# Router ranks from one subtraction, sums that are shared, and a new order for a Mamba and mixture-of-experts layer

## The chip, the cores and the metric

The kernel runs on one core of a Trainium2 chip, as one program of some 14,000 instructions. The core has five engines that run side by side, each with its own queue of instructions in a fixed order: TensorE (PE in the profile, with its weight loads as PEld), VectorE (DVE), ScalarE (ACT), GpSimd (POOL) and SyncE (SP), which here only starts transfers. An engine takes its queue in order, so an instruction that waits holds everything behind it on that engine. TensorE writes its results into PSUM, the small accumulator memory; everything else lies in SBUF, the working memory of 128 partitions, or in device memory. The metric is the device time of one execution in microseconds (us).

## The reference

The layer takes x of 4 sequences x 1024 tokens x 128 features in float32. It has two halves, each followed by a residual sum and a layer normalization.

```python
# first half: a selective state-space mixer (Mamba), per sequence
xr, z = split(x @ W_in.T)                       # 256 channels each
xs    = silu(causal_conv4(xr) + conv_b)
dt_r, b, c = split(xs @ W_x.T)                  # 64, 16, 16
dt    = softplus(dt_r @ W_dt.T + b_dt)
h_t   = exp(dt_t * a) * h_{t-1} + (dt_t * x_t) * b_t   # 16 states for each channel
y_t   = sum_s(h_t * c_t) + D * x_t
x     = layernorm(x + (y * silu(z)) @ W_out.T)
# second half: 8 experts, the best 2 for each token
scores = x @ Wr + br
weights = softmax over the two largest scores   # the lower index wins a tie
out    = sum_e weights[e] * (gelu(x @ W1[e] + b1[e]) @ W2[e] + b2[e])
x      = layernorm(x + out)
```

## The kernel before

**Units and rounds.** The tokens are cut into ten units (`UNITS`, line 42): pieces of one sequence of 512 tokens, at the start two of 256, at the end one of 384 and one of 128. A unit is handled as chunks of 128 tokens, n of them (4, 3, 2 or 1). The first nine units make eight sparse rounds for the experts (`ROUNDS`; round 0 has the two units of 256, each other round one unit, so rounds 1 to 6 have 512 tokens and round 7 has 384); the last unit of 128 tokens is dense: it goes through all eight experts.

**The mixer.** For each unit `project`, `select` and `softplus` make the inputs of the scan. Then `step` (line 802) runs 16 times, once for each state: TensorE spreads b over the partitions (line 824), VectorE multiplies it with dt*x (line 861), ScalarE makes the decay a (line 847), VectorE runs the recurrence with one scan for each half of the channels (line 880), POOL multiplies the result h with c (line 895, tile hc) and TensorE adds it up in y (line 905). h has 2 buffers and hc has 3, so a scan can wait for POOL's product of an earlier step. `finish_mixer` (line 949) gates y, projects it, normalizes it into the tile acc, has SP copy acc into a second tile, twin (line 1017), and computes the router scores.

**Router.** Still in `finish_mixer`, and all on VectorE: `score` (line 1056) adds the bias and takes the largest score of each token. `ranks` (line 1067) compares all 8 x 8 pairs of scores of a token: greater, or equal with the other's index lower (the constant triangle `before`). Four operations make a 0 or 1 for each pair, a sum over the 8 others gives each expert's rank, and ranks 0 and 1 give the mask. `weigh` (line 1096) takes the exponentials (ScalarE, line 1093) times the mask, sums them, takes the reciprocal, and multiplies. `most` and `first_only` belong to the way the bias b1 is folded into W1: row 0 of the transposed tokens is replaced by ones.

**Dispatch.** `dispatch` (line 1128) works on a round. TensorE counts tokens for each expert; `blocks` (line 1172, VectorE) turns the counts into blocks of 128 slots, with running sums over the 8 experts made from a product with the triangle `upto` and a sum, and finds which expert owns each block; `places` (line 1201) finds the slots of each token's best and second expert, with a product and a sum for each; `weights` (line 1230) does the same for the two router weights and writes them as a 129th column of acc (best) and twin (second). Then POOL scatters each chunk twice, acc by the best slot and twin by the second, into a slot table in device memory (line 1262, two scatters for a chunk, eight for a round of 512 tokens). The slot tables are set to zero once near the start, by four transfers from SP (`clear`, line 506).

**Experts.** `experts` (line 1322) loads four blocks of 128 slots at a time (xb), transposes them on TensorE, copies them to SBUF as xq, multiplies with W1 (line 1290), applies gelu on ScalarE (line 1303), multiplies with W2 (line 1314), scales with the weight column into yb and stores them. A round of 512 tokens has 15 blocks, round 7 has 13. For rounds below `LATE` the copy xq (line 1350) and the scaling yb (line 1426) run on ScalarE, for the others on VectorE (lines 1359 and 1428). `combine` gathers the two results of each token with an indirect DMA of POOL that adds into acc (line 1495), `store` normalizes and writes. `dense` does the last unit.

**What sets the order.** Every piece of work is put into a `Plan` (line 77) with an engine, an estimated cost, what it reads and writes, a place (in units of one step of 512 tokens) and an urgency. `order` (line 147) simulates the engines with these costs and sorts all pieces into one list; the queues follow this list. The constants in lines 22 to 49 are places, urgencies and switches of this planner: `B_AT` to `BC_URG` place the step's parts, `PREP` to `SSTEP` and `PREP_OF` the preparation of a unit, `D_AT` and `D_OF` the dispatch, `X_AT` and `X_OF` the experts, `C_AT` and `C_OF` the combining, `Z_AT` the clearing of the slot tables, `W1_AT` and `W2_AT` the fetch of the expert weights. Work marked `port=True` on VectorE and POOL is planned one at a time; for work marked `beside` (POOL's scatters and gathers) `BESIDE` and `PATIENCE` (lines 27 and 28, read in lines 185 to 189) say when it may be started:

```python
if op["beside"] and needy:
    if port[0] == "DVE" and max(t, port[1]) <= port[2] - BESIDE:
        t = max(t, port[1])
    else:
        t = max(t, known + PATIENCE)
```

## Time and profile before

| | |
|---|---|
| median of 16 runs | 796.25 us (794.18 to 798.0) |
| the profiled execution: its own time / its span | 798.54 us / 796.8 us |
| TensorE busy | 658.7 us (83%), 4594 matmuls |
| VectorE busy | 657.5 us (83%), 1036 instructions |
| ScalarE busy | 558.0 us (70%), 843 instructions |
| GpSimd busy | 532.6 us (67%), 637 instructions |
| TensorE clock granted, mean | 0.912 of full |
| last scan ends | at 733.9 us of the span |

The profile gives busy times by engine and by groups of instructions (line of the kernel, engine, operation, output<-input, shape, count, busy us, mean ns of one), tables of busy time by stretch of the span, who waited for whom, a timeline of each engine, and the chain of work that ended last, followed back from the end. A busy share is a mean over stages with different limits; a wait counts only on the engine that sets the end of its stage. A busy TensorE in these records is not one at its peak, since its matmuls are pipelined.

### The profile page before, as it was taken

The numbers are of one execution on the slowest core, as the hardware profiler recorded it, in microseconds if no ns is written. First come the engines' busy times: TensorE is split into PE (matmuls) and PEld (weight loads), VectorE is DVE, ScalarE is ACT, GpSimd is POOL, SyncE is SP. The second block draws the span as 40 slices with busy tenths as digits, with TensorE's granted clock in tenths as the row PEclk, the third lists the DMA queues.
The fourth block names the chain that finished last, engine by engine and source line by source line (L and its number), as shares of the span: only waits on it lengthen the run. The fifth ranks groups of instructions, "written<-read, shape, count | busy, mean of one in ns | idle before, by whom it ended". The sixth has DMA issues, their size and how long they took to land. (4 is left out here: it accounts for less than half of the span.)

```text
span 796.8 us, 14284 instructions
## 1 busy us (share of the span) xinstructions
PE 658.7 (83%) x4594; PEld 563.0 (71%) x4594; DVE 657.5 (83%) x1036; ACT 558.0 (70%) x843; POOL 532.6 (67%) x637
## 2 busy tenths in 40 slices
PE   5557838669997999799987996999789988888885
PEld 4446526358875987598766874988588977777784
DVE  2698998999989998999989989998979997984322
ACT  2853865827867886778777888787867867675553
POOL 4356545576656897479938795769686886975604
PEclk9765967859997999889998998899999999999998
DMA  6952313347424664266524633555355555566652
GB/s 190 232 144 56 104 46 102 106 126 230 142 60 127 191 175 118 67 172 183 140 66 128 203 75 116 155 179 161 81 155 175 140 148 177 144 144 178 149 160 36
DMA packets 106120, 109.20 MB, mean 137 GB/s; under 512 B 9640, under 2 KB 72152, under 8 KB 106048
## 3 DMA queue, kind: packets, MB, share of 16 engines
q1 hardware_dynamic: 94384, 99.44, 43.4%
q0 software_dynamic: 11248, 8.33, 5.9%
q8 instruction: 38, 0.62, 0.3%
q10 hardware_dynamic: 416, 0.53, 0.2%
q14 instruction: 34, 0.28, 0.1%
HBM read 87.96 MB, written 18.27 MB: 133 GB/s over the span
## 5 line engine op out<-in xcount | busy, mean ns | idle before, releaser
L895 POOL TENSOR_TENSOR hc<-h,cc 128x512 f32<-128x512 f32 (+3 forms) x320 | 358.1, 1219 | 158.7 <-DVE h L880 34.0
L905 PE MATMUL y<-ident,hc 128*128 128x128 f32 x1024 | 172.7, 293 | 49.7 <-POOL hc L895 47.5
L880 DVE TENSOR_TENSOR_SCAN h<-a,state,u 128x512 f32<-128x512 f32 (+3 forms) x192 | 185.4, 1000 | 20.4 <-POOL hc L895 7.3
L847 ACT ACTIVATE a<-dt,nega 128x1024 f32<-128x1024 f32 (+3 forms) x160 | 152.9, 974 | 66.2 <-DVE h L880 60.2
L861 DVE TENSOR_TENSOR u<-dtx,u 128x1024 f32<-128x1024 f32 (+3 forms) x160 | 162.2, 1014 | 22.9 <-PE u L824 10.7
L905 PEld LDWEIGHTS y<-ident,hc 128*128 128x128 f32 x1024 | 124.8, 149 | 78.1 <-POOL hc L895 72.2
L1314 PE MATMUL ph<-w_sb,ht 128*128 x944 | 131.5, 292 | 24.3 <-ACT ht L1303 24.2
L1314 PEld LDWEIGHTS ph<-w_sb,ht 128*128 128x128 f32 x944 | 121.7, 206 | 28.7 <-ACT ht L1303 28.3
L880 DVE TENSOR_TENSOR_SCAN h<-a,u 128x512 f32<-128x512 f32 (+1 forms) x128 | 132.9, 1074 | 10.1 <-POOL hc L895 3.6
L1290 PE MATMUL ph<-xq,w 128*128 128x128 f32 x944 | 125.8, 283 | 15.4 <-DVE pick L1233 3.2
L243 ACT ACT_TABLE_LOAD x105 | 134.7, 1283 | 3.6 <-PEq L1657 1.8
L1290 PEld LDWEIGHTS ph<-xq,w 128*128 128x128 f32 x944 | 116.2, 197 | 21.3 <-issue 6.4
L1495 POOL DMA_INDIRECT acc<-ys_slots,slot_i x62 | 97.9, 1579 | 41.8 <-DVE acc L1555 24.5
L824 PE MATMUL u<-ident,bt 128*128 128x128 f32 x512 | 89.4, 290 | 10.6 <-DVE h L880 10.6
L1303 ACT ACTIVATE ht<-ph 128x512 f32<-128x512 f32 x118 | 66.0, 597 | 23.6 <-PE ph L1290 22.7
L824 PEld LDWEIGHTS u<-ident,bt 128*128 128x128 f32 x512 | 65.2, 148 | 20.7 <-DVE h L880 13.3
L1426 ACT ACTIVATE yb<-ph,xb 128x128 f32<-128x128 f32 x105 | 37.2, 363 | 46.9 <-PE ph L1314 42.4
L1262 POOL DMA_INDIRECT xs_slots<-acc,slot_i x31 | 33.8, 1090 | 46.9 <-DVE twin L1241 13.2
L613 PE MATMUL pxc<-xt,taps 128*128 128x512 f32 (+3 forms) x160 | 61.2, 531 | 3.2 <-ACT xt L603 2.6
L613 PEld LDWEIGHTS pxc<-xt,taps 128*128 128x128 f32 x160 | 30.1, 203 | 24.8 <-issue 17.5
L745 ACT ACTIVATE sq<-ex,shift 128x1024 f32<-128x1024 f32 (+3 forms) x40 | 38.0, 973 | 7.2 <-DVE q L753 6.5
L1262 POOL DMA_INDIRECT xs_slots<-twin,slot_i x31 | 35.6, 1149 | 6.8 <-issue 5.7
(140 smaller groups left out, 709.7 us busy)
## 6 DMA issues: line engine op xcount, KB each, us to landing
w<-w_dram SPq DMA_DIRECT2D x118, 256.0 KB, 3.1
cc<-cd SPq DMA_DIRECT2D x96, 256.0 KB, 3.5
xb<-xs_slots SPq DMA_DIRECT2D x24, 258.0 KB, 3.8
ys_slots<-yb SPq DMA_DIRECT2D x24, 256.0 KB, 2.4
cc<-cd SPq DMA_DIRECT2D x32, 128.0 KB, 2.9
cc<-cd SPq DMA_DIRECT2D x16, 192.0 KB, 3.1
w_sb<-in_w_dram SPq DMA_DIRECT2D x8, 256.0 KB, 4.8
w_own<-in_w_dram SPq DMA_DIRECT2D x8, 256.0 KB, 4.9
```

Source lines behind the costliest of these rows:

```text
L243: load(table)
L613: nc.tensor.matmul(pp()[:, :t_n], taps[:, k, c * P : (c + 1) * P], xt()[:, k : k + t_n], start=(k == 0), stop=(k == KC - 1),)
L824: nc.tensor.transpose(u_sb[:, bank, k * P : (k + 1) * P], bt()[:, k, s : s + 1].to_broadcast([P, P]), ident,)
L847: lambda: nc.scalar.activation(a()[:, :, :t_n], dt()[:, :, :t_n], AF.Exp, scale=nega[:, s : s + 1]),
L861: nc.vector.tensor_tensor((u_sb[:, 1:3, :t_n] if bank else u_sb[:, 1::-1, :t_n]), dtx()[:, :, :t_n], u_sb[:, bank : bank + 1, :t_n].to_bro ...
L880: nc.vector.tensor_tensor_scan(h()[:, c, :t_n], a()[:, c, :t_n], u_sb[:, (1, bank)[c], :t_n], 0.0 if first == 0 else carry()[:, s, c : c + 1],
L895: nc.gpsimd.tensor_tensor(hc()[:, c, :t_n], h()[:, c, :t_n], cc()[:, :t_n], ALU.mult)
L905: nc.tensor.matmul(y()[:, k, c * P : (c + 1) * P], hc()[:, c, k * P : (k + 1) * P], ident, is_transpose=True, start=False, stop=(s == NS - 1),
L1262: ins = nc.gpsimd.indirect_dma_start(out=rd["xs"]()[:, :], out_offset=bass.IndirectOffsetOnAxis(ap=slot_i()[:, k, st["chunk"] + c : st["ch ...
L1290: nc.tensor.matmul(ph()[:, k * P : (k + 1) * P], w()[:, k * P : (k + 1) * P], xt()[:, width], start=True, stop=True, skip_group_check=True,)
L1314: nc.tensor.matmul(py, ht[:, k, :], w2_sb[:, bass.ds(e, 1), k * DM : (k + 1) * DM].rearrange("p o d -> p (o d)"), start=(k == 0), stop=(k ...
L1495: nc.gpsimd.indirect_dma_start(out=acc()[:, c, :DM], out_offset=None, in_=ys()[:, :], in_offset=bass.IndirectOffsetOnAxis(ap=slot_i()[:, k ...
```

## The change

- `ranks`: the difference other - own is taken once and compared with a constant `least`, which is 0 where the other's index is lower and the smallest normal number elsewhere. That replaces greater, equal, product and sum: two operations for four. The tile eq goes.
- `weigh`: compares the rank itself with 2 instead of reading the mask, and puts the reciprocal of the sum straight into the weight column of acc: the best expert's exponential is exp(0) = 1, so its weight is the reciprocal. It now writes a part of acc.
- `blocks`: the running sums over 8 experts come from one scan (times one, plus the count) instead of a product with `upto` and a sum. `upto` goes, a tile of ones comes.
- `places`: the two products go into one tile, and one sum covers both slots.
- `weights`: only the second weight is left, one product and one sum for each unit.
- `LATE` goes from 7 to 6: round 6 too has its xq copies and its output scaling on VectorE.
- The planned costs of these pieces and most constants of the planner are other numbers: a new order of all queues.

```diff
@@ -23,21 +23,21 @@
 GATHER, SCATTER = 1.85, 1.35
 N_B = 2
 SCAN_ORDER = 1, 0
-B_AT, B_URG = 3.6, 29.9
-BESIDE = -6.2
-PATIENCE = 0.2
+B_AT, B_URG = 4.3, 38.4
+BESIDE = -3.0
+PATIENCE = -3.9
 N_RUSH = 0
-X_AT, X_STEP, X_URG, C_AT, C_URG, D_AT = 1.9, 2.66, 6.2, 4.0, -1.0, -1.9
-A_AT, A_URG, BC_AT, BC_URG = -0.8, -2.3, 4.2, 15.8
-PREP, SEL, SOFT, SSTEP = 25.4, 5.3, -0.1, 2.7
-L_URG = -1.0
-URG, URG2, URG3, URG4 = 52.0, 191.1, 18.3, 0.8
-Z_AT, W2_AT, W1_AT, W1_STEP = 11.2, 0.0, 6.8, 3.5
-
-PREP_OF = (-6.7, -1.0, -10.0, 9.5, 1.2, 0.0, -3.0, 5.6, -5.2, 6.9, -3.9, 3.0)
-D_OF = (7.9, -3.5, -6.5, 3.3, 6.5, 4.7, -8.1, 5.3, 4.5, 1.7)
-X_OF = (-1.9, -7.6, 2.1, 1.3, 0.5, 0.4, 0.8, -16.1, 6.0, -2.5)
-C_OF = (-0.2, 5.0, -3.5, -1.3, 8.3, 3.3, 21.1, -2.6, 2.7, 9.1)
+X_AT, X_STEP, X_URG, C_AT, C_URG, D_AT = 2.0, 2.67, 6.2, 2.3, -0.7, -5.0
+A_AT, A_URG, BC_AT, BC_URG = -3.9, -0.9, 2.6, 13.8
+PREP, SEL, SOFT, SSTEP = 25.4, 8.6, -1.6, 7.4
+L_URG = 0.2
+URG, URG2, URG3, URG4 = 61.4, 108.8, 18.4, 1.7
+Z_AT, W2_AT, W1_AT, W1_STEP = 25.9, 0.4, 6.8, 3.1
+
+PREP_OF = (-10.5, 3.7, -10.0, 9.5, 2.6, 0.1, -1.2, 5.6, -5.2, 6.9, 2.2, 1.3)
+D_OF = (7.9, -1.6, -6.5, -9.3, 2.6, 3.6, -8.5, 5.0, 5.0, 1.7)
+X_OF = (-0.7, -10.0, 2.1, 1.3, 0.5, 0.4, 2.3, -10.7, 4.2, -7.3)
+C_OF = (4.2, 6.7, -4.4, -7.9, 5.2, 3.4, 22.2, -1.9, 1.2, 9.4)
 
 UNITS = [
     (0, 0, 256), (0, 256, 256), (0, 512, 512), (1, 0, 512), (1, 512, 512), (2, 0, 512), (2, 512, 512), (3, 0, 512), (3, 512, 384), (3, 896, 128),
@@ -46,8 +46,10 @@
 
 DENSE = [(9,)]
 
-LATE = 7
+LATE = 6
 EPS = 1e-5
+
+TINY = 2.0**-126
 TOPK = 2
 
 
@@ -365,7 +367,11 @@
 
 
     before = triangle([P, E, E], [[1, E], [-1, E]], 0, 0, "before")
-    upto = triangle([P, E, E], [[1, E], [-1, E]], 1, 0, "upto")
+
+    least = const.tile([P, E, E], F32, name="least")
+    nc.vector.tensor_scalar(least, before, -TINY, TINY, op0=ALU.mult, op1=ALU.add)
+    one_e = const.tile([P, E], F32, name="one_e")
+    nc.gpsimd.memset(one_e, 1.0)
     sooner = triangle([P, P], [[1, P]], 0, -1, "sooner")
 
     w2_sb = const.tile([P, E, PF], F32, name="w2_sb")
@@ -1046,7 +1052,6 @@
         full = [P, n, E, E]
         sc = sb(small, [P, NTC, E], "sc", 2, f"sc_{i}")
         gt = sb(small, [P, NTC, E, E], "gt", 1, f"gt_{i}")
-        eq = sb(small, [P, NTC, E, E], "eq", 1, f"eq_{i}")
         top = sb(small, [P, NTC], "top", 2, f"top_{i}")
         tot = sb(small, [P, NTC], "tot", 2, f"tot_{i}")
         rd, c0 = st["round"], st["chunk"]
@@ -1067,11 +1072,9 @@
         def ranks():
             each = sc()[:, :n].unsqueeze(3).to_broadcast(full)
             other = sc()[:, :n].unsqueeze(2).to_broadcast(full)
-            g, q = gt()[:, :n], eq()[:, :n]
-            nc.vector.tensor_tensor(g, other, each, ALU.is_gt)
-            nc.vector.tensor_tensor(q, other, each, ALU.is_equal)
-            nc.vector.tensor_tensor(q, q, before.unsqueeze(1).to_broadcast(full), ALU.mult)
-            nc.vector.tensor_tensor(g, g, q, ALU.add)
+            g = gt()[:, :n]
+            nc.vector.tensor_tensor(g, other, each, ALU.subtract)
+            nc.vector.tensor_tensor(g, g, least.unsqueeze(1).to_broadcast(full), ALU.is_ge)
             nc.vector.tensor_reduce(rank()[:, cs], g, AX.X, ALU.add)
             nc.vector.tensor_scalar(mask()[:, cs], rank()[:, cs], float(TOPK), None, op0=ALU.is_lt)
             nc.vector.tensor_tensor(
@@ -1083,10 +1086,10 @@
 
         plan.add(
             "DVE",
-            0.7 + 0.43 * n,
+            0.6 + 0.3 * n,
             ranks,
             [sc, top],
-            [gt, eq, (rank, i), (mask, i), sc],
+            [gt, (rank, i), (mask, i), sc],
             port=True,
         )
         act(
@@ -1095,14 +1098,16 @@
 
         def weigh():
             w = rw()[:, cs]
-            nc.vector.tensor_tensor(w, mask()[:, cs], sc()[:, :n], ALU.mult)
+            nc.vector.scalar_tensor_tensor(
+                w, rank()[:, cs], float(TOPK), sc()[:, :n], op0=ALU.is_lt, op1=ALU.mult
+            )
             nc.vector.tensor_reduce(tot()[:, :n], w, AX.X, ALU.add)
-            nc.vector.reciprocal(tot()[:, :n], tot()[:, :n])
-            nc.vector.tensor_tensor(
-                w, w, tot()[:, :n].unsqueeze(2).to_broadcast([P, n, E]), ALU.mult
-            )
-
-        plan.add("DVE", 0.8, weigh, [(mask, i), sc], [(rw, i), tot], port=True)
+
+            best = acc()[:, :n, DM:DW]
+            nc.vector.reciprocal(best.rearrange("p c o -> p (c o)"), tot()[:, :n])
+            nc.vector.tensor_tensor(w, w, best.to_broadcast([P, n, E]), ALU.mult)
+
+        plan.add("DVE", 0.8, weigh, [(rank, i), sc], [(rw, i), tot, (acc, "w")], port=True)
         if not rd["sparse"]:
             st["xq"] = xq = sb(ffn, [P, QUAD * P], "xq", 2, f"xqd_{i}")
             act(
@@ -1157,14 +1162,13 @@
 
         over = sb(small, [P, E, MAXC], "over", 1, f"over_{r}")
         nb = sb(small, [P, E], "nb", 1, f"nb_{r}")
-        pre = sb(small, [P, E, E], "pre", 1, f"pre_{r}")
         ends = sb(small, [P, E], "ends", 1, f"ends_{r}")
         base = sb(small, [P, E], "base", 1, f"base_{r}")
         done = sb(small, [1, MAXB, E], "done", 1, f"done_{r}")
         whose = sb(small, [1, MAXB], "whose", 1, f"whose_{r}")
         whose_i = sb(small, [1, MAXB], "whose_i", 2, f"whose_i_{r}", U32)
         pos = sb(small, [P, MAXC, E], "pos", 1, f"pos_{r}")
-        pick = sb(small, [P, MAXC, E], "pick", 2, f"pick_{r}")
+        pick = sb(small, [P, TOPK, MAXC, E], "pick", 2, f"pick_{r}")
         slot = sb(small, [P, TOPK, MAXC], "slot", 1, f"slot_{r}")
         slot_i = sb(small, [P, TOPK, MAXC], "slot_i", 2, f"slot_i_{r}", U32)
         pe(0.25 * (n_c + 1), counts, [mask], [cnt], holds=[over, base, whose_i, pos, slot, slot_i])
@@ -1178,10 +1182,9 @@
                 ALU.is_gt,
             )
             nc.vector.tensor_reduce(nb(), over()[:, :, :n_c], AX.X, ALU.add)
-            nc.vector.tensor_tensor(
-                pre(), upto, nb().unsqueeze(1).to_broadcast([P, E, E]), ALU.mult
-            )
-            nc.vector.tensor_reduce(ends(), pre(), AX.X, ALU.add)
+            nc.vector.tensor_tensor_scan(
+                ends(), one_e, nb(), 0.0, op0=ALU.mult, op1=ALU.add
+            )
             nc.vector.tensor_tensor(base(), ends(), nb(), ALU.subtract)
             nc.vector.tensor_tensor(
                 done()[:, :n_b],
@@ -1195,7 +1198,7 @@
             )
 
         plan.add(
-            "DVE", 1.6, blocks, [cnt], [over, nb, pre, ends, base, done, whose, whose_i], port=True
+            "DVE", 1.15, blocks, [cnt], [over, nb, ends, base, done, whose, whose_i], port=True
         )
 
         def places():
@@ -1209,45 +1212,37 @@
             )
             for k in range(TOPK):
                 nc.vector.scalar_tensor_tensor(
-                    pick()[:, :n_c],
+                    pick()[:, k, :n_c],
                     rank()[:, :n_c],
                     float(k),
                     pos()[:, :n_c],
                     op0=ALU.is_equal,
                     op1=ALU.mult,
                 )
-                nc.vector.tensor_reduce(slot()[:, k, :n_c], pick()[:, :n_c], AX.X, ALU.add)
+            nc.vector.tensor_reduce(slot()[:, :, :n_c], pick()[:, :, :n_c], AX.X, ALU.add)
             nc.vector.tensor_copy(slot_i()[:, :, :n_c], slot()[:, :, :n_c])
 
-        plan.add("DVE", 1.2, places, [cnt, base, rank], [pos, pick, slot, slot_i], port=True)
+        plan.add("DVE", 1.0, places, [cnt, base, rank], [pos, pick, slot, slot_i], port=True)
         rd["slot"], rd["whose"] = slot_i, whose_i
         rd["xs"], rd["ys"] = xs_fixed[r % 2], ys_fixed[r % 2]
 
         for i in rd["units"]:
             st = units[i]
-            copies = st["acc"], st["twin"]
-
-            def weights(st=st, copies=copies, n=size(i)[1]):
+            twin = st["twin"]
+
+            def weights(st=st, twin=twin, n=size(i)[1]):
                 cs = slice(st["chunk"], st["chunk"] + n)
-                for k in range(TOPK):
-                    nc.vector.scalar_tensor_tensor(
-                        pick()[:, cs],
-                        rank()[:, cs],
-                        float(k),
-                        rw()[:, cs],
-                        op0=ALU.is_equal,
-                        op1=ALU.mult,
-                    )
-                    nc.vector.tensor_reduce(
-                        copies[k]()[:, :n, DM : DW].rearrange("p c o -> p (c o)"),
-                        pick()[:, cs],
-                        AX.X,
-                        ALU.add,
-                    )
-
-            plan.add(
-                "DVE", 0.8, weights, [rank, rw], [pick, *((t, "w") for t in copies)], port=True
-            )
+                nc.vector.scalar_tensor_tensor(
+                    pick()[:, 0, cs], rank()[:, cs], 1.0, rw()[:, cs], op0=ALU.is_equal, op1=ALU.mult
+                )
+                nc.vector.tensor_reduce(
+                    twin()[:, :n, DM:DW].rearrange("p c o -> p (c o)"),
+                    pick()[:, 0, cs],
+                    AX.X,
+                    ALU.add,
+                )
+
+            plan.add("DVE", 0.4, weights, [rank, rw], [pick, (twin, "w")], port=True)
         earlier = []
         for i in rd["units"]:
             st = units[i]
```

## The prediction

> **What bounds the kernel now.** I read the busy shares in 40 slices first, then the table of 20 us stretches, then who waited for whom, the chain that ended last, and at the end VectorE's groups by shape. The slices (tenths busy, 20 us each):
>
> ```profile
> PE   5557838669997999799987996999789988888885
> DVE  2698998999989998999989989998979997984322
> ```
>
> VectorE (DVE) stands at 8 or 9 from slice 3 to about 720 us, then falls to 4, 3, 2; TensorE stays at 8 to the end. So there are two regimes. Two stretches of the table, one of each (busy us of PE, PEld, DVE, ACT, POOL out of 20, then clock, DMA share, GB/s):
>
> ```profile
> 180.00:200.00 20.00, 19.48 (x167) 18.57 (x168) 18.90 (x16) 15.90 (x20) 13.04 (x12) 1.00 0.77 233
> 740.00:760.00 20.00, 15.90 (x133) 14.85 (x132) 7.70 (x33) 13.28 (x22) 11.53 (x8) 1.00 0.69 160
> ```
>
> From 160 to 660 us the 25 stretches hold 458.2 us of VectorE in 500, or 91.6%, and most of what is missing is gaps of about 0.1 us between dependent instructions. The scans run back to back: a step of 512 tokens is one product and two scans, 3.9 us. What VectorE really waited for between 100 and 735 us is short (wait: us, times, longest):
>
> ```profile
> DVE h L880 <- POOL hc L895: 10.8, 3, 6.4
> DVE u L861 <- PE u L824: 8.6, 8, 3.3
> DVE sc L1057 <- PE pr L1036: 4.7, 4, 3.0
> ```
>
> So until about 720 us the time is VectorE's instruction stream, and any instruction taken out of it ahead of that point moves everything behind it. The chain shows what comes after: the scatters of the last sparse round on POOL's queue, then TensorE's expert matmuls, then a chain through VectorE's ranks of the dense unit.
>
> ```profile
> 728.17 0.97 POOL xs_slots L1262
> 729.16 1.70 POOL hc L895 x4
> 738.74 2.07 PE ph L1290 x16
> 748.89 0.14 DVE eq L1072
> 749.06 0.23 DVE eq L1073
> 750.07 0.73 DVE xq L1359
> ```
>
> The last two fences say where the change bites: on VectorE's stream nearly everywhere, and once in the tail, where the transposed tokens (xq) wait behind the ranks.
>
> **The change, part by part.** VectorE's groups by shape (count, busy us, mean ns, idle):
>
> ```profile
> L1071 DVE TENSOR_TENSOR gt<-sc 128x256 f32<-128x256 f32 x6 | 2.5, 409 | 0.0
> L1072 DVE TENSOR_TENSOR eq<-sc 128x256 f32<-128x256 f32 x6 | 2.5, 417 | 0.0
> L1073 DVE TENSOR_TENSOR eq<-eq,before 128x256 f32<-128x256 f32 x6 | 5.8, 959 | 0.2
> L1074 DVE TENSOR_TENSOR gt<-gt,eq 128x256 f32<-128x256 f32 x6 | 2.5, 425 | 0.2
> L1184 DVE TENSOR_REDUCE ends<-pre 128x8 f32<-128x64 f32 x8 | 1.8, 220 | 0.3
> L1211 DVE SCALAR_TENSOR_TENSOR pick<-rank,pos 128x32 f32<-128x32 f32 x14 | 2.7, 192 | 0.5
> L1241 DVE TENSOR_REDUCE twin<-pick 128x4 f32<-128x32 f32 x6 | 1.1, 189 | 0.2
> ```
>
> *Ranks.* Four operations become two. In the timeline of unit 7 the four run from 643.65 to 645.33, 1.68 us; two dependent ones of 0.42 with their gap take 0.45 each, 0.90. So 0.78 us is saved in each of six 512-token units (4.7). In the same way: 1.19 to 0.66 in the two 256-token units (1.1), 1.49 to 0.80 in the one of 384 (0.7), 0.90 to 0.52 in the dense one (0.4, on the chain above). Together 6.8 us.
>
> *Blocks.* The product with "upto" and its sum take 0.52 us (657.45 to 657.97). The scan of 8 has no row. Nearest are the scans of 512, 256 and 128: (1208 - 673)/256 = 2.09 ns an element, and 468 - 120 x 2.09 = 217 ns at 8. Bounds: 155 ns (the 673 ns row taken down the same slope) and 468 ns (the whole row of 128). I take 217 with a gap of 0.04, 0.26 us, because the row of 128 is the nearest in size: 8 x 0.26 = 2.1 us; bounds 0.1 and 2.6.
>
> *Places.* Product, sum, product, sum take 0.89 us (658.93 to 659.82). Two products at 0.22 and one sum over 64 elements (the row of L1184, 220 ns, 0.26 with its gap) make 0.70: 8 x 0.19 = 1.5 us.
>
> *Weights.* One product and one sum go, 0.45 us a unit of 512 (660.78 to 661.23), 0.41 and 0.40 for the smaller: 6 x 0.45 + 0.41 + 2 x 0.40 = 3.9 us.
>
> *Weigh.* A product becomes a scalar_tensor_tensor (180 to 190 ns, 10 times: +0.1). Writing the reciprocal into a column of acc costs what L1241 pays for such a column, 188 ns against L1219's 186: nothing. The write could add a wait: the copy of acc to twin reads the same tile, and behind the reciprocal VectorE's next scans would queue, which POOL and TensorE wait for. In the last sparse unit that copy is issued at 706.88 and lands about 3.4 us later; the sum of weights starts at 714.85. It is hidden by 4.5 us, and would cost that difference only if the weights came within 3.4 us of the copy's issue. The mask is no longer needed by weigh, but the counts still need it: nothing. In the prologue one triangle (0.17 and 0.29 us of POOL) goes, and a product of 64 elements and a memset come, before VectorE's idle 10.9 us at 14 to 25 us: nothing; without that idle, 0.2 us.
>
> Sum of the arithmetic: 6.8 + 2.1 + 1.5 + 3.9 - 0.1 = 14.2 us off VectorE.
>
> *Stalls inside the removed lines.* The six L1073 average 959 ns though the median of the line is 424, and single long ones fall on L1072 (1369 ns at 139.95), L1073 (2673 at 478.14), L1181 (1142 at 324.31), L1098 (1979 at 568.94), L1076 (2021 at 645.79): a different line each time, while POOL multiplies. What is recorded above the undisturbed price in the removed lines is 1.2 + 3.6 + 1.8 = 6.6 us. I count none of it: the wait belongs to the moment and falls on the neighbour. Bounds: 0 and 6.6. The Trainium skill, page "SBUF — State Buffer", section "Who interferes with whom", says a VectorE instruction with two SBUF inputs and a GpSimd instruction that reads SBUF exclude each other for whole instructions, and tensor_reduce never contends. That speaks against a bonus, since the subtraction, the comparison and the products left still have two such inputs; this trace agrees on the reduce (L1075 never above 422 ns). By the rule the sum stays 14.2, without it 20.8.
>
> *LATE from 7 to 6.* Round 6's 15 output scalings and 4 xq copies go from ScalarE to VectorE: 15 x 0.351 + 3 x 0.81 + 0.65 = 8.4 us (rows of round 7, L1428 and L1359). By ScalarE's timeline 2 scalings and 2 xq fall before 691.8, where unit 8's scans end (2.3 us), 6 and 1 up to 720 (2.9), the rest where VectorE idles anyway (6.4 us for POOL at 723.7 to 730, and more behind it). So 5.2 us are on VectorE's path. ScalarE loses 15 x 0.367 + 3.0 = 8.5 us; TensorE waited 0.86 and 1.43 us for its gelu at 716 and 722, of which I give back half, 1.2. Cost 4.0; bounds -2.3 (the relief alone) and 8.4.
>
> *The new order.* The constants shift when preparation, scatters, gathers and combines come up in every queue; nothing in this trace prices that. SP's four clearing transfers (24 to 42 us, 0.4 us each to issue, about 1 MB per slot table) come later; they must land before the first scatter at 149 us, and have over 100 us of room. BESIDE and PATIENCE change which of POOL's products and indirect DMAs go first. I take 0 for the order; at best it returns VectorE's three waits behind scatters (13.3 us, first rival), at worst it adds five (17.9, third rival).
>
> *Through to the end.* VectorE fills 91.6% of the long stretch; where it waits, a saving just ahead is swallowed. I let 8% of 14.2 go, 1.1 us. The sum: -14.2 + 1.1 + 4.0 = -9.1 us. The profiled execution took 798.54 us (its span 796.8 and 1.74 around it), 2.3 above the median of the 16 runs; the 9.1 are 1.1% of it and I take them from the median: 796.25 - 9.1 = 787.2 us.
>
> **The rivals.**
>
> *The order gains as well (0.15).* VectorE waits for POOL behind a block of scatters in three rounds: 3.57 us at 589 (round 5), 3.35 at 671 (round 6), 6.40 at 724 (round 7), together 13.3. If an order takes them all away: 787.2 - 13.3 = 773.9; 770 to 781. For it: in round 5 POOL first stood 3.73 us on a scatter that waited for the twin's weights, which now come earlier. Against: the eight scatters have to be issued somewhere.
>
> *TensorE or POOL takes the place (0.11).* Only half of 14.2 arrives: 796.25 - 7.1 + 4.0 = 793.2; 791 to 794.6. For it: TensorE was busy all 20 us of 460 to 480 and of 500 to 520. Against: a TensorE busy in the records isn't at its peak, and its waits on hc (47.5 us) end with VectorE's work.
>
> *Slower: POOL's queue (0.21).* Eight scatters hold POOL for 8.0 to 10.3 us with the products behind them, and VectorE ran out of free h buffers in three of eight rounds. If the new PATIENCE puts the scatters ahead of the products in the other five too, at round 5's 3.57 each: 787.2 + 17.9 = 805.1. It decides from (796.25 - 787.2)/3.57 = 2.5, so three further rounds (797.9). For it: the planner's scatter cost isn't touched, but the patience is cut by 4.1. Against: a shorter VectorE group also brings its scans sooner.
>
> *No change that shows (0.05).* LATE at its full 8.4 and half of the arithmetic lost: 796.25 - 7.1 + 8.4 = 797.6.
>
> **How the numbers follow.** The forecast, 781 to 793 around 787.2, gets 0.48; it rests on plain counts in a stream that is full, and is uncertain by LATE and the order. About 0.2% (1.6 us) is what a measurement of this kernel can tell from no change. Faster: 0.48 + 0.15 + 0.11 = 0.74; within 0.2%: 0.05; slower: 0.21. The range reaches into the second and the fourth case: 773 (the order gains nearly all) to 803 (four stalled rounds, 801.5, and a little), leaving out about 0.05 below and 0.08 above.
>
> **What would show it.** Right: VectorE's busy time near 652 us (657.5 - 14.2 + 8.4); two 0.42 us operations between score and rank sum; the scan of 8 near 0.22 us; the last scan 8 to 14 us before its present end at 733.9; L1359 and L1428 with 8 and 28 instructions. Wrong: VectorE's waits on POOL well above 14.6 us (10.8 for hc, 3.8 for the state copy), the stretches 160 to 660 below 90% busy, or the distance from the last scan to the end above today's 63 us by as much as the scans gained; then the saving went into POOL's queue or the expert tail.

## The result and the profile after

The changed kernel takes 805.35 us (median of 11 runs, 802.61 to 806.75); the kernel before takes 796.75 us beside it (59 runs). The ratio is 1.0104, with a 95% interval of 1.0094 to 1.0114: 1% slower, where the prediction said 787.2 us and 773 to 803. The experiments below ran on several chips, on which the kernel before took 796.8, 797.61, 807.21, 807.93 or 808.79 us, so ratios to it are compared and not microseconds, unless the runs are of one chip. A ratio doesn't carry over exactly either: on the slower chips one stretch of the new order is some 5 us longer and the same stretch of the old order is not, as is seen below.

The busy shares of the changed kernel in 40 slices of its span of 803.0 us:

```profile
PE   5557939759995998998979997899878988988886
DVE  1698998999998999697899999899779986976322
```

VectorE's row has a 6 at 321 to 341 us and at 662 to 683, and 7s at 361 to 381 and from 562 to 602; in the row of before two 7s, at 578 to 598 and 637 to 657, are all that breaks the 8s and 9s of that stretch. The table of 20 us stretches has them (columns as for the kernel before: busy us of PE, PEld, DVE, ACT, POOL, then clock, DMA share, GB/s):

```profile
320.00:340.00 20.00, 18.74 (x157) 17.36 (x156) 12.64 (x25) 11.92 (x25) 14.12 (x22) 1.00 0.58 164
580.00:600.00 20.00, 15.84 (x109) 13.42 (x107) 12.60 (x11) 13.94 (x27) 15.67 (x20) 0.91 0.60 170
```

VectorE's waits in the changed kernel (wait: us, times, longest):

```profile
DVE h L886 <- POOL state L926: 12.5, 2, 7.0
DVE h L886 <- POOL hc L901: 11.2, 6, 6.5
DVE u L867 <- PE u L830: 4.6, 7, 1.8
```

The scans' wait for POOL is 23.7 us now and was 14.6. The shortened code did become shorter, though (groups by shape: count, busy us, mean ns, idle):

```profile
L1076 DVE TENSOR_TENSOR gt<-sc 128x256 f32<-128x256 f32 x6 | 2.7, 444 | 0.0
L1077 DVE TENSOR_TENSOR gt<-gt,least 128x256 f32<-128x256 f32 x6 | 4.3, 721 | 0.2
L1185 DVE TENSOR_TENSOR_SCAN ends<-one_e,nb 128x8 f32<-128x8 f32 x8 | 1.4, 174 | 0.3
L1222 DVE TENSOR_REDUCE slot<-pick 128x8 f32<-128x64 f32 x7 | 1.5, 220 | 0.2
```

Two operations stand where four stood, the scan of 8 elements takes 174 ns, the shared sum 220. VectorE's busy time is 657.3 us against 657.5, because round 6's copies and scalings came to it and small instructions became longer (see the last points below); the last scan ends at 744.2 us, 10.3 later than before. So the question is not what the arithmetic costs but where the order of the queues lost more than the arithmetic gained.

### The profile page after: what moved, and what is told of

It reads as the page before. It is cut to its first block, busy times and chain, and to the rows that moved or that the text cites. A ratio compares the mean times of both kernels' runs of the same rounds, so it can differ in the third digit from the quotient of the medians.

```text
span 803.0 us, 14220 instructions
## 1 busy us (share of the span) xinstructions
PE 665.1 (83%) x4594; PEld 567.0 (71%) x4594; DVE 657.3 (82%) x1002; ACT 535.6 (67%) x814; POOL 532.2 (66%) x636
## 5 line engine op out<-in xcount | busy, mean ns | idle before, releaser
L911 PE MATMUL y<-ident,hc 128*128 128x128 f32 x1024 | 177.2, 299 | 57.8 <-POOL hc L901 56.1
L911 PEld LDWEIGHTS y<-ident,hc 128*128 128x128 f32 x1024 | 127.1, 152 | 89.2 <-POOL hc L901 85.1
L1309 PE MATMUL ph<-w_sb,ht 128*128 x944 | 127.8, 285 | 18.9 <-ACT ht L1298 18.8
L1285 PE MATMUL ph<-xq,w 128*128 128x128 f32 x944 | 127.9, 287 | 16.0 <-ACT xq L1345 3.7
L1285 PEld LDWEIGHTS ph<-xq,w 128*128 128x128 f32 x944 | 118.5, 201 | 24.2 <-ACT xq L1345 6.2
L1309 PEld LDWEIGHTS ph<-w_sb,ht 128*128 128x128 f32 x944 | 117.8, 199 | 23.1 <-ACT ht L1298 22.3
L1490 POOL DMA_INDIRECT acc<-ys_slots,slot_i x62 | 100.3, 1618 | 42.0 <-DMA ys_slots<-yb 27.0
L830 PEld LDWEIGHTS u<-ident,bt 128*128 128x128 f32 x512 | 66.7, 150 | 19.4 <-DVE h L886 13.7
L1257 POOL DMA_INDIRECT xs_slots<-acc,slot_i x31 | 32.1, 1035 | 51.1 <-ACT ex L727 13.3
L1421 ACT ACTIVATE yb<-ph,xb 128x128 f32<-128x128 f32 x90 | 31.3, 363 | 42.6 <-PE ph L1309 32.1
L619 PEld LDWEIGHTS pxc<-xt,taps 128*128 128x128 f32 x160 | 30.1, 204 | 23.7 <-issue 17.2
```

Source lines behind the costliest of these rows:

```text
L619: nc.tensor.matmul(pp()[:, :t_n], taps[:, k, c * P : (c + 1) * P], xt()[:, k : k + t_n], start=(k == 0), stop=(k == KC - 1),)
L830: nc.tensor.transpose(u_sb[:, bank, k * P : (k + 1) * P], bt()[:, k, s : s + 1].to_broadcast([P, P]), ident,)
L911: nc.tensor.matmul(y()[:, k, c * P : (c + 1) * P], hc()[:, c, k * P : (k + 1) * P], ident, is_transpose=True, start=False, stop=(s == NS - 1),
L1285: nc.tensor.matmul(ph()[:, k * P : (k + 1) * P], w()[:, k * P : (k + 1) * P], xt()[:, width], start=True, stop=True, skip_group_check=True,)
L1309: nc.tensor.matmul(py, ht[:, k, :], w2_sb[:, bass.ds(e, 1), k * DM : (k + 1) * DM].rearrange("p o d -> p (o d)"), start=(k == 0), stop=(k ...
L1490: nc.gpsimd.indirect_dma_start(out=acc()[:, c, :DM], out_offset=None, in_=ys()[:, :], in_offset=bass.IndirectOffsetOnAxis(ap=slot_i()[:, k ...
```

## The experiments

**The arithmetic and the order, each without the other.** The first kernel has the new sums, but the planner's constants, costs and declared reads and writes of before, so that the queues of TensorE, ScalarE and SyncE are those of before row for row; `LATE` is 7. The second has the new order, with `LATE` at 6, and the old sums.

```diff
--- changed kernel
+++ new sums in the old order (core of it)
-B_AT, B_URG = 4.3, 38.4
-BESIDE = -3.0
-PATIENCE = -3.9
+B_AT, B_URG = 3.6, 29.9
+BESIDE = -6.2
+PATIENCE = 0.2
...
-LATE = 6
+LATE = 7
...
-            0.6 + 0.3 * n,
+            0.7 + 0.43 * n,
```

> The new arithmetic (two operations for ranks, scan of 8, shared sum, best weight by the reciprocal) with every constant, cost and declaration of the planner as in the kernel before, so that the order of all queues is the one before; LATE stays 7. Theory A (the arithmetic is worth what was predicted, the new order lost it): 796.75 less 14.2 less some 8% of that swallowed = 783.7, between 781 and 787, VectorE busy about 643 us. Theory B (the saved VectorE time turns into waits for POOL and TensorE in any order): 791 to 797, with VectorE's named waits on POOL up by 5 us or more from 14.6.

```diff
--- changed kernel
+++ old sums in the new order (core of it)
-            nc.vector.tensor_tensor(g, other, each, ALU.subtract)
-            nc.vector.tensor_tensor(g, g, least.unsqueeze(1).to_broadcast(full), ALU.is_ge)
+            nc.vector.tensor_tensor(g, other, each, ALU.is_gt)
+            nc.vector.tensor_tensor(q, other, each, ALU.is_equal)
+            nc.vector.tensor_tensor(q, q, before.unsqueeze(1).to_broadcast(full), ALU.mult)
+            nc.vector.tensor_tensor(g, g, q, ALU.add)
```

> The other corner: the order of the changed kernel, but ranks by four operations, running sums by product and sum, one sum for each slot, and the best weight by its own product and sum (right behind the reciprocal). Theory A (arithmetic and order simply add): 805.4 + 13.1 = 818.5, between 815 and 822. Theory B (in this order VectorE's arithmetic is not what binds): 805 to 810.

Measured, with the kernel before at 796.8 us on the chip of the two (796.75 beside the changed kernel):

| | old order | new order |
|---|---|---|
| old sums | 796.8 us | 819.14 us, ratio 1.0281 [1.0261, 1.03] |
| new sums | 783.14 us, ratio 0.9817 [0.98, 0.9834] | 805.35 us, ratio 1.0104 [1.0094, 1.0114] |

The right column has `LATE` at 6; the next experiment takes that apart. The table adds up: the sums are worth 13.7 us in the old order and 13.8 in the new one, the order costs 22.3 and 22.2. The new sums in the old order are the fastest kernel of this study, 1.8% faster than the kernel before.

**`LATE`.** Round 6's four xq copies and 15 output scalings stay on ScalarE, at the places that the new order gives them.

```diff
-                if r < LATE:
+                if r <= LATE:
```

> The changed kernel with the same list of work, but round 6's 4 xq copies and 15 output scalings are emitted on ScalarE at the same places (8.4 us off VectorE, 8.5 us onto ScalarE). If these pieces, in VectorE's queue ahead of the last scans and waiting for TensorE, are what makes the last unit late (the last scan 10 us later than before): 797 to 802, the last scan about 4 to 8 us earlier. If they are hidden, or ScalarE is then late instead: 804 to 808.

Measured: 805.86 us, ratio 1.0108 [1.0091, 1.0124]; the changed kernel has 1.0104. Moving 19 instructions from one engine to the other made no difference, though VectorE's busy time differs by 5.7 us (651.6 against 657.3). The trace shows what hides them: without them VectorE waits 6.81 us for POOL at 735.9, behind round 7's scatters; with them it waits 1.37 there.

This kernel has the same 983 VectorE instructions as the new sums in the old order, so the two show the order alone. Unit by unit (from the start of one unit's gating to the next unit's, the last column to the end of the span), in us:

| stretch | units 0-2 | 3 | 4 | 5 | 6 | 7 | 8 | 9 | behind it |
|---|---|---|---|---|---|---|---|---|---|
| old order | 207.9 | 80.8 | 81.5 | 80.0 | 84.6 | 81.1 | 66.5 | 39.4 | 60.1 |
| new order | 207.9 | 77.9 | 88.3 | 83.8 | 79.5 | 91.6 | 70.1 | 48.2 | 55.6 |

The spans are 21.2 us apart. Units 4 and 7 are 6.8 and 10.5 us longer, 17.3 together; the other columns go both ways (unit 9 is 8.8 longer, unit 6 is 5.1 shorter) and add 3.9.

**Single constants, and the waits by themselves.** In the changed kernel VectorE's largest waits for POOL stand behind blocks of scatters: 6.53 us at 337.1 (round 2), 6.99 at 587.2 (round 5), 5.48 at 677.1 (round 6). Six kernels tried to take them away. Two have planner settings put back, the two for scatters or all of them, and the whole list is then sorted anew; four have POOL's queue alone rewritten, in the new order and in the old one.

```diff
-BESIDE = -3.0
-PATIENCE = -3.9
+BESIDE = -6.2
+PATIENCE = 0.2
```

> The changed kernel with only BESIDE and PATIENCE back at -6.2 and 0.2, the planner then sorts anew. If the scatters and gathers that now go ahead of POOL's products are the loss: VectorE's waits on POOL fall from 23.7 us to 15 or less and the time to 795 to 799. If the loss is spread over the order: 802 to 812.

> The changed kernel with every constant of the planner and LATE as before; its new planned costs and declarations stay, so the planner sorts anew (about half of the queue rows stand elsewhere than in the kernel before). If the constants of the change make its order slow: 780 to 788, near the 783.1 of the kept order. If what matters is that an order was fitted to one list of work, and any newly sorted one loses: 792 to 810.

For the next four POOL's queue is rewritten after the sorting: each scatter behind one following product, or the whole block behind the two following products.

```diff
     order = plan.order(NEAR, loth=LOTH)
+    order = spread_scatters(order)
...
+            out.append(op)
+            if held and op.get("kind") == "product":
+                out.append(held.pop(0))
```

> The changed kernel with only POOL's queue altered: a round's scatters are no longer one block, each one is put behind a following product hc, until something needs the scattered rows. All other queues are row for row the same. If VectorE's waits behind the block of scatters (22.8 us here against about 11 in the kept order) are the loss: those waits fall below 12 us and the time to 793 to 798. If the waits only mark an order that is late for other reasons: 803 to 807.

> The same alteration of POOL's queue on the kept order with the new arithmetic (783.1 us, some 11 us of waits behind scatters in rounds 5 to 7). If those waits cost what they last: 774 to 779. If experts then start later by as much, or the products that follow pile up: 782 to 788.

> The changed kernel with only POOL's queue altered, less than when each scatter was put behind a product: the whole block of a round's scatters moves behind the two products that followed it, which POOL can do in the 4 to 8 us that it stood idle in front of the first scatter. The last scatter is later by 0 to 2.5 us. If POOL's idle time ahead of the block is the loss: ratio 0.997 to 1.005, VectorE's waits behind scatters from 22.8 to about 15. If any delay of the scatters is paid by TensorE: 1.010 to 1.020.

> The same move on the kept order with the new arithmetic. By the first reading of the run above: 0.974 to 0.980. By the second: 0.983 to 0.995.

| kernel | ratio to before [95%] |
|---|---|
| changed, old `BESIDE` and `PATIENCE` | 1.05 [1.0455, 1.0544] |
| changed, all old constants, sorted anew | 1.0928 [1.0864, 1.0992] |
| changed, scatters spread | 1.0184 [1.0136, 1.0231] |
| new sums in the old order, scatters spread | 1.0046 [1.0021, 1.007] |
| changed, scatters behind two products | 1.0216 [1.0187, 1.0246] |
| new sums in the old order, scatters behind two products | 1.0209 [1.018, 1.0238] |

None is faster than what it was made from, and what became of the waits differs. (The scans' waits for POOL are 23.7 us in the changed kernel and 12.0 in the new sums in the old order.)

- With old `BESIDE` and `PATIENCE` the waits stay, 23.0 us. The loss lies at the end: from unit 9's gating to the end of the span it takes 87.6 us, where the changed kernel takes 54.7.
- With all old constants and the changed costs the waits fall to 6.6 us and the kernel is 9.3% slower than the one before: this set of constants goes with the costs it was made for.
- With the block behind two products the waits stay in the new order (23.8 us) and grow in the old one (28.3).
- With the scatters spread they stay in the old order (12.6 us, and 3.2 more behind a scatter's spacer). On the chip of that run the old order reaches unit 7's gating at 618.1 us (a kernel mixed below), this one at 634.4.
- With the scatters spread in the new order they fall from 23.7 to 2.6 us. That chip is a slower one, on which the changed kernel itself was not run; but a kernel mixed below has the new order up to unit 7 there, and both reach unit 7's gating at 640.5 us. So spreading is not shown to cost anything in the new order; the 23.7 us of waits went, and nothing was gained.

In the last kernel VectorE waits elsewhere instead, for TensorE's spread of b (waits of the changed kernel with the scatters spread):

```profile
DVE u L867 <- PE u L830: 20.5, 12, 9.8
DVE u L867 <- remote: 8.3, 2, 6.2
```

The first line was 4.6 us. A reading that no run tests by itself: a later scatter makes the experts' pieces of that round later in TensorE's queue, which has spreads of b behind them (round 2's first transpose starts at 359.8 us here, at 354.0 in the unspread order on the same chip). Two products are some 2.5 us of POOL for a round, and cost 3.9% in the old order. So moving POOL's queue alone, in these two ways, bought nothing back.

**A third buffer for h**, so that the scans could run on while POOL scatters, paid with one of the four buffers of cc (the spread c from device memory):

```diff
-        cc = sb(scan, [P, T], "cc", 4, f"cc_{i}_{s}")
+        cc = plan.buf("cc", 4, lambda: scan.tile([P, T], F32, tag="cc", name=f"cc_{i}_{s}", bufs=3))
...
-        h = sb(scan, [P, NDC, T], "h", 2, f"h_{i}_{s}")
+        h = plan.buf("h", 2, lambda: scan.tile([P, NDC, T], F32, tag="h", name=f"h_{i}_{s}", bufs=3))
```

> The changed kernel, all queues row for row the same, but the scan's result h has three buffers in place of two (and cc three in place of four, to make room). VectorE can run one step, 3.9 us, further ahead of POOL's products. If its waits behind the scatters (6.5, 7.0 and 5.5 us in rounds 2, 5 and 6 and smaller ones) are lost for good: each shrinks by up to 3.9, the sum from 22.8 to some 11, and the ratio to the kernel before goes from 1.010 to 0.994 to 1.000. If TensorE or POOL set the pace there and VectorE only waits for them: 1.005 to 1.012.

> The same three buffers on the kept order with the new arithmetic (ratio 0.982 so far, some 11 us of such waits, most in rounds 5 to 7). If the waits are lost for good: 0.972 to 0.977. If not: 0.980 to 0.985.

Measured: 1.1294 [1.1272, 1.1316] and 1.084 [1.0812, 1.0867]. The swap buried what it was to show. SyncE's queue, which fetches cc, waits for a free buffer of it (the old order with the swap):

```profile
SPq L839 <- POOL hc L899: 263.9, 56, 25.4
SPq L839 <- POOL state L924: 239.8, 72, 15.7
```

Without the swap these lines read 98.5 and 151.6 us, and what stands behind the fetches in that queue comes late: TensorE waits 9.2 us for weights w (none before) and 18.0 for the blocks xb (2.6 before), and POOL 19.7 us for cc itself (1.4 before). Whether a third h alone helps stays open.

**Mixing the two orders.** The two lists hold the same 3,330 pieces of work, so a kernel can follow one list up to a unit's last scan and the other for the rest. At those places behind units 6 and 7 the lists are 5 and 14 pieces apart.

```diff
+    new = [op["n"] for op in plan.order(NEAR, loth=LOTH)]
+    old = [int(n) for n in OLD_ORDER.split()]
+    first = old[: old.index(last) + 1]
+    order = [plan.ops[n] for n in first + [n for n in new if n not in set(first)]]
```

> The new sums, round 6 on ScalarE as in the two kernels that are mixed; all work in the old order up to the last scan of unit 6, what is left in the new order (at that place the two lists differ by 5 of 2,164 pieces). The two pure orders took 783.1 and 805.9, and unit 6's gating began at 534.8 and 537.4 in them. Theory 'local': each stretch keeps its price whatever goes before, so the old start returns 2.6 and the rest is lost: 803.3. Rival 'early': the new order's loss is laid in by what it leaves undone up to unit 6 (gathers, experts' pieces): with the old start 783 to 787. Rival 'any seam': each departure from a list that was fitted as a whole costs 2 to 5%, as the other reordered kernels did: over 810.

> The mirror: the new order up to unit 6's last scan, then the old. 'Local': 783.1 + 2.6 = 785.7. 'Early': 800 to 806. 'Any seam': over 800.

> The same with the change of order one unit later, behind unit 7's last scan; unit 7's gating began at 615.9 in the old order and 629.0 in the new. 'Local': 805.9 - 13.1 = 792.8, so unit 7 alone carries 10.5. 'Early': 783 to 787. 'Any seam': over 810.

> The mirror: the new order up to unit 7's last scan, then the old. 'Local': 783.1 + 13.1 = 796.2. 'Early': 800 to 806. 'Any seam': over 800.

| order up to / behind | us | ratio [95%] | 'local' | stretch of unit 7 |
|---|---|---|---|---|
| unit 6: old / new | 814.11 | 1.0081 [1.0056, 1.0106] | 1.008 | new, 94.4 us |
| unit 7: old / new | 804.27 | 0.9962 [0.994, 0.9984] | 0.995 | old, 84.4 us |
| unit 6: new / old | 810.11 | 1.0029 [1.0008, 1.0051] | 0.986 | old, 84.3 us |
| unit 7: new / old | 820.66 | 1.0156 [1.0113, 1.0198] | 0.999 | new, 98.5 us |

('Local' is the expected time as a ratio to 796.8.) The first two rows came out as expected. The last two are 1.6 to 1.7% above it: on this chip the new order's start is longer, with unit 6's gating at 542.6 and 542.0 us where it was 537.4, while the old order's is not (533.9 and 533.7 against 534.8), and the old order's units 8 and 9 take 8 and 5 us more than on the first chip. But the rows that differ in unit 7's stretch alone, the first from the second and the fourth from the third, are 9.84 and 10.55 us apart, with either order around it; the marks of the first chip had said 10.5. That the stretch of unit 7 carries some 10 of the 22 us is shown.

What happens there (the line numbers are 146 higher, since these kernels carry the list): VectorE in the kernel that follows the new order from unit 7 on (start, duration, operation, idle before it), from the end of the dispatch:

```profile
567.57 0.19 DVE L1384 TENSOR_REDUCE twin<-pick 128x4 f32<-128x32 f32 x1
567.67 1.21 DVE L1032 TENSOR_TENSOR_SCAN h<-a,u 128x512 f32<-128x512 f32 x1
568.92 1.23 DVE L1013 TENSOR_TENSOR u<-dtx,u 128x1024 f32<-128x1024 f32 x1
570.25 2.33 DVE L1032 TENSOR_TENSOR_SCAN h<-a,u 128x512 f32<-128x512 f32 x2
572.69 1.23 DVE L1013 TENSOR_TENSOR u<-dtx,u 128x1024 f32<-128x1024 f32 x1
580.87 2.33 DVE L1032 TENSOR_TENSOR_SCAN h<-a,u 128x512 f32<-128x512 f32 x2 [6.95 <-POOL state L1072]
590.71 0.17 DVE L632 SCALAR_TENSOR_TENSOR rstd_o<-mv_o,rstd_o 128x4 f32<-128x4 f32 x1 [7.51 <-ACT rstd_o L626]
```

And in the one that keeps the old order up to unit 7's end:

```profile
568.37 0.19 DVE L1384 TENSOR_REDUCE twin<-pick 128x4 f32<-128x32 f32 x1
568.48 0.95 DVE L905 SCALAR_TENSOR_TENSOR q<-sq,ex 128x768 f32<-128x768 f32 x1
569.53 0.96 DVE L905 SCALAR_TENSOR_TENSOR q<-sq,q 128x768 f32<-128x768 f32 x1
...
575.46 0.96 DVE L905 SCALAR_TENSOR_TENSOR q<-sq,q 128x768 f32<-128x768 f32 x1 [0.34 <-ACT sq L897]
576.46 0.96 DVE L918 SCALAR_TENSOR_TENSOR dt<-q,dt 128x768 f32<-128x768 f32 x1
577.45 0.96 DVE L932 TENSOR_TENSOR dtx<-dt,xs 128x768 f32<-128x768 f32 x1
578.33 1.22 DVE L1013 TENSOR_TENSOR u<-dtx,u 128x1024 f32<-128x1024 f32 x1
582.13 2.33 DVE L1032 TENSOR_TENSOR_SCAN h<-a,u 128x512 f32<-128x512 f32 x2 [2.59 <-POOL hc L1047]
```

In both POOL makes no product for 16 us (562.3 to 578.2 and 565.2 to 580.8) while the router's results are made and the eight scatters issued. In the old order VectorE has 5.7 us of the next unit's softplus (q, dt, dtx) to do in that gap; in the new order none of it: it fills its two h buffers and stops. The preparation's chain on TensorE and ScalarE then runs at 580 to 591, and VectorE waits for ScalarE behind it as well (7.51).

In the changed kernel itself the first wait is there and the second is not; rstd_o is long instead (VectorE's timeline of the changed kernel):

```profile
587.22 2.33 DVE L886 TENSOR_TENSOR_SCAN h<-a,u 128x512 f32<-128x512 f32 x2 [6.99 <-POOL state L926]
589.47 2.78 DVE L486 SCALAR_TENSOR_TENSOR rstd_o<-mv_o,rstd_o 128x4 f32<-128x4 f32 x1
602.92 3.00 DVE L759 SCALAR_TENSOR_TENSOR q<-sq,q 128x768 f32<-128x768 f32 x2
```

Unit 7's stretch in the new sums in the old order, and in the new order with round 6 on ScalarE, both on one chip (columns as above):

```profile
534.80:615.90 81.10, 74.18 (x553) 65.45 (x552) 72.53 (x102) 63.33 (x98) 64.96 (x73) 0.96 0.54 148
537.40:629.00 91.60, 80.30 (x577) 69.10 (x575) 78.53 (x101) 63.59 (x100) 68.68 (x76) 0.94 0.48 133
```

Of the 10.5 us between these two, 4.5 are idle time of VectorE (the wait for POOL alone is 6.99 against 2.31), and 6.0 are busy time with the same pieces of work: rstd_o takes 2.76 us where it took 0.16, and the four q take 5.7 where they took 3.8. Two of the four stand beside POOL's products now and take 1.85 and 1.98 us; in the gap each took 0.96. The clock is no rival: the changed kernel has 91.1 us in this stretch at the same granted clock as the old order, 0.96, and in unit 4's stretch the new order has 1.00 against 0.96.

The same sum over q, dt and dtx (those that start between POOL's last product before a scatter block and its first behind it), for all eight rounds of the first three kernels in us, with VectorE's wait for POOL behind the block:

| round | 0 | 1 | 2 | 3 | 4 | 5 | 6 | 7 |
|---|---|---|---|---|---|---|---|---|
| before: preparation in the gap / wait | 4.9 / 0 | 7.3 / 0 | 7.3 / 0 | 7.3 / 0 | 7.4 / 0 | 5.7 / 3.57 | 2.5 / 3.35 | 0 / 6.40 |
| new sums, old order | 4.9 / 0 | 7.3 / 0 | 7.3 / 0 | 7.4 / 0 | 7.4 / 0 | 5.7 / 2.31 | 2.5 / 2.90 | 0 / 5.49 |
| changed kernel | 7.3 / 0 | 6.1 / 1.17 | **0 / 6.53** | 7.3 / 0 | 7.3 / 1.25 | **0 / 6.99** | 2.5 / 5.48 | 0 / 1.37 |

The two gaps that the new order left without preparation, rounds 2 and 5, lie in the stretches of units 4 and 7. They are two of the three that grew most; the third is unit 9's, whose gap (round 7) has no preparation in either order, and behind which 4.5 of its 8.8 us come back. The changed kernel's round 7 waits little because round 6's moved scalings and copies lie in that gap.

**Putting single stretches back.** Three more mixes, with the list changed for two stretches or for one:

```diff
+    for i in range(NU):
+        source = old if i in (4, 7) else new
+        for n in source[: source.index(last_scan[i]) + 1]:
+            taken.setdefault(n)
```

> The new order, but the stretches of units 4 and 7 (from the last scan of the unit before to their own) in the old one. These are the two stretches in which the new order has no VectorE work of the next unit's preparation while POOL is free of products for the scatters (0 us of q, dt and dtx in the gaps at 318.8 and 567.2, against 7.3 and 5.9 us in the old order; in all gaps with 7 us of it VectorE waits nothing). By the marks they take 88.2 and 91.6 us in the new order, 81.5 and 81.1 in the old. Theory 'cover': 6.7 + 10.5 come back: a ratio of 1.0108 - 0.0216 = 0.989. Rival 'the waits alone': 6.5 + 7.0 less what the old order waits there (2.6): 0.997. Rival 'any seam': over 1.011.

> The old order, but the stretches of units 3 and 6 in the new one, the two that were shorter there by the marks (77.9 against 80.8 us, 79.5 against 84.7). If each stretch keeps its price: 0.9817 - 0.0102 = 0.9715, the fastest of all. Rival 'borrowed': they are shorter only because the stretch before left work undone or done early: 0.982 to 0.99. Rival 'any seam': over 1.0.

> The old order, but the stretch of unit 7 in the new one, which takes the preparation out of round 5's gap. 'Cover': the 10.5 us of the marks, 0.9817 + 0.0132 = 0.995, with VectorE's wait behind that scatter block going from 2.6 to 7 us and a further wait for ScalarE's rstd_o behind it. Rival 'the waits alone': 0.987. Rival 'any seam': over 1.01.

| kernel | ratio [95%] | stretch 3 | 4 | 5 | 6 | 7 |
|---|---|---|---|---|---|---|
| new, units 4 and 7 old | 1.0103 [1.0053, 1.0152] | 84.8 | 88.7 | 85.1 | 79.4 | 86.0 |
| old, units 3 and 6 new | 0.9943 [0.9922, 0.9963] | 85.5 | 82.2 | 86.3 | 80.4 | 84.8 |
| old, unit 7 new | 1.0029 [0.9996, 1.0062] | 80.8 | 81.5 | 80.1 | 84.7 | 95.5 |

The third behaved as the missing cover says, and lost somewhat more than the marks had given. Its waits in the stretch are the ones expected, one of POOL and one of ScalarE behind it (VectorE's timeline of that kernel):

```profile
582.45 2.33 DVE L1032 TENSOR_TENSOR_SCAN h<-a,u 128x512 f32<-128x512 f32 x2 [6.98 <-POOL state L1072]
593.38 0.16 DVE L632 SCALAR_TENSOR_TENSOR rstd_o<-mv_o,rstd_o 128x4 f32<-128x4 f32 x1 [8.60 <-ACT rstd_o L626]
```

Over the nine kernels with the new sums, round 6 on ScalarE and no queue rewritten, unit 7's stretch is 81.1 to 86.0 us in the old order (five kernels) and 91.6 to 98.5 in the new one (four). The first kernel missed its 0.989: its unit 7 came back (86.0), and VectorE waits nothing for POOL in round 2's gap, but units 3 and 4 take 84.8 and 88.7. So unit 4 had its preparation back, lost its wait and was no shorter than the changed kernel's 88.2; on another of the slower chips the new order's unit 4 takes 92.8 and 93.6, and on this one it was not run. The waits that stand there instead lie behind a seam: behind unit 3 the lists are 29 pieces apart, and VectorE waits 5.06 us for TensorE's u at 291.8 and 8.94 for y at 382.3. That the seam makes them is the likely reading; no run tests it. The second missed too, with a wait behind the same seam (6.02 us for u at 293.0): unit 6's gating is at 543.6 us, against 535.4 in the third on the same chip. That the new order's units 3 and 6 could be had for nothing by such a mix is refuted.

So: the order costs 22 us, shown; unit 7's stretch is 10 of them, shown; that the missing preparation is what makes it long fits the traces of all kernels, with the waits foretold in one of them, but no run moved the preparation and nothing else, and what fills the 10 us differs from chip to chip (two waits on the slower ones; one wait and longer instructions on the first). For unit 4 only the traces speak (6.8 us longer, with one wait of 6.53), and the one kernel that put its stretch back did not make it shorter. Which constant took the preparation out of the two gaps stays open. With `D_AT`, `D_OF` and `URG2` put back the planner's list is the changed kernel's row for row, so it is none of these three; `SEL`, `SOFT` and `PREP_OF` are among the others that moved.

## Why the prediction was wrong, point by point

- **The step that failed: "I take 0 for the order".** It measures +22.2 us in the new arithmetic. The bounds given beside it, -13.3 and +17.9, did not hold it, and the range ended at 803. Some 10 of the 22 us lie in unit 7's stretch, where the new order left VectorE without preparation while POOL scatters. The profile of before could have said more than that nothing prices it: VectorE's waits behind the scatters were nothing in the five rounds with 4.9 to 7.4 us of preparation in POOL's gap, and 3.57, 3.35 and 6.40 in the three with 5.7, 2.5 and 0. That `SEL` and `SOFT`, which place the preparation, move was in the diff.
- **The arithmetic, 14.2 us.** Right in its sum: 13.7 and 13.8 us of time, and of VectorE's busy time 14.6 in the old order and 13.9 in the new. Little was swallowed: 13.7 us of the 14.2 arrived, where 13.1 were expected.
- **The scan of 8**: 174 ns in the changed kernel, 217 taken, 155 to 468 given. (In the new sums in the old order two of the eight are long, 1086 and 1093 ns.) A term too large by 0.04 us in each of eight rounds. The shared sum: 220 taken, 220 measured.
- **The stalls inside the removed lines: 0 of 6.6 counted.** Right. Long ones still occur in the code that is left: L1077 averages 721 ns for 256 elements, of which the undisturbed ones take 424. The Trainium skill's rule that was set against the bonus ("SBUF — State Buffer", section "Who interferes with whom") agrees: the rank sum, a reduce, averages 420 ns at 256 elements in the changed kernel.
- **`LATE`, +4.0.** Mis-sized: nothing that can be measured (ratios 1.0104 and 1.0108). The step asked where VectorE idles in the order of before; in the new order the gap of round 7 takes 5.4 us of the moved work.
- **The prologue and weigh's write, 0.** Nothing contradicts it.
- **The rival "POOL's queue".** It had the sign, and its 805.1 us came near by luck. It was to be five further rounds with 3.57 us each, from scatters put ahead of products. There is one new long wait (round 2, 6.53), two short new ones (rounds 1 and 4, 1.17 and 1.25), two longer ones (round 5, 6.99 for 3.57, and round 6, 5.48 for 3.35) and a shorter one (round 7, 1.37 for 6.40): 22.8 us for 13.3. And the gap in POOL's products in round 2 is 14.3 to 15.3 us in all three kernels; what changed is VectorE's work inside it. It had the largest chance of the four rivals, 0.21.
- **What was to show it.** VectorE's busy time, "near 652", is 657.3. The order alone adds 8.7 us to it, with the same 983 instructions (651.6 against 642.9): rstd_m and rstd_o take 4.9 and 4.4 us against 1.5 and 1.6, to name the two largest. The moved work adds 5.7 where 8.4 were counted. Of the three signs named for wrong one came: "waits on POOL well above 14.6 us", 23.7. The stretches from 160 to 660 us are 90.1% busy, just above the 90 named, and the last scan lies 58.8 us ahead of the end, not more than 63.

## What to carry to other kernels

Cost a change of arithmetic and a change of order apart, and run each alone: here the first was worth 13.7 us as counted, and the second took 22 back. Before a block on an in-order queue is moved, look at what the other engine does during that block, and whether it still does it afterwards; the table of work in the gap against wait behind it is quickly made. And don't price a wait in a fitted order by its length: four kernels with POOL's queue alone rewritten gained nothing, not even the one that lost nearly all of these waits.

## What was not expected of the hardware

- A short VectorE instruction can become many times longer: rstd_m, 4 elements wide in the largest units, averages 148 ns in one order and 493 ns in the other, for the same ten instructions; in the changed kernel one rstd_o takes 2.78 us, at 589.47, while two of POOL's products run beside it (589.74 to 592.22).
- One buffer of cc less, with one of h more, made the old order 10% slower: SyncE's waits for a free buffer of cc rose from 250.1 to 503.7 us, and TensorE's loads behind them came late.
- Chips differ in places: the old order's first 530 us are the same on those where the kernel before took 807 to 809 us (unit 6's gating at 533.7 to 535.4 against 534.8); unit 8's stretch is where they lose, with 74.2 to 77.1 us in the old order against 66.5. Over that stretch the granted clock of TensorE is 1.00 in the new sums in the old order and 0.91 in the kernel with units 3 and 6 new, with the same busy time of VectorE (columns as above). All kernels run on those chips with a trace of this stretch in the old order are mixed or have POOL's queue rewritten, so what the chip does and what the mixing does are not separated, and the second line is of that kernel's slowest run (812.53 us, median 805.34):

```profile
615.90:682.40 66.50, 61.76 (x505) 56.14 (x506) 56.98 (x105) 51.17 (x93) 58.20 (x77) 1.00 0.63 158
628.40:705.50 77.10, 65.96 (x500) 60.86 (x501) 57.04 (x105) 51.31 (x93) 58.42 (x77) 0.91 0.52 136
```
